# A two-layer graph-attention and expert network: first biases, filler, slots in a row and weight fetches

## The chip, the cores and the metric

One core of one Trainium2 chip runs the whole program. The metric is the device time of one execution in microseconds (us). In the text PE or TensorE is the matrix engine, DVE or VectorE the vector engine, ACT or ScalarE the engine of activation functions, POOL or GpSimd the engine that issues the indirect DMAs, and SP or SyncE the engine that issues the plain DMAs. A name such as L1454 is a line of the kernel before.

## What is computed

Two layers, each an attention over a graph of N = 2708 nodes with D = 256 features, followed by a mixture of 8 experts of which each node uses two:

```python
# layer 0
x = x + gnn0(layernorm(x), adj)      # q k v, masked softmax, elu
x = x + ffn0(layernorm(x))           # top 2 of 8 experts, H = 1024, own norm scale and shift per expert
# layer 1
x = x + gnn1(layernorm(x), adj)      # H = X W + b, scores s_src + s_dst, masked softmax, alpha H
x = x + ffn1(layernorm(x))           # top 2 of 8 experts, H = 512

# one expert
h = gelu(x_e @ W1[e] + b1[e])        # exact gelu
y = h @ W2[e] + b2[e]                # summed over the two experts with the router's weights
```

All inputs and outputs are 32 bit floats; the masks come as a 2708 x 2708 matrix of integers.

## The kernel before

The nodes are cut into NT = 22 tiles of 128 rows. Layer 0's attention goes through six blocks of up to 512 queries (`layer0_attention`); for each of the 22 key tiles of a block it makes scores (L545), exponentials on ScalarE (L557), a product with the mask on VectorE (L560, whose results `p` lie in six buffers), and the sums with the values (L609). At the end of a block the sums are copied (L634, half of them on VectorE), and the remaining steps of a tile (elu, residual, norm, routing) are done piece by piece beside later work through a `Line` of generators.

Routing (`route`) writes each row twice, once for each of its two experts, with an indirect DMA of POOL (L1207) into the DRAM tensor `disp`, sorted by expert. The experts' part is a list of slots of 128 rows of one expert each. There are SURE = 43 slots that are always used, and at most SLOTS = 50. Which expert a slot has is computed at run time (`place`), as a row number (`token_row`) and weight rows (`weight_row`). A slot needs:

- its rows `xg` and their targets and weights `who`, by five DMAs of SP (`fetch_rows`, L1395 and L1401), up to ROWS_AHEAD = 5 slots ahead;
- its expert's weights in one of RING = 4 buffers `ring`, by an indirect DMA of POOL (`fetch_weights`, L1368), AHEAD = 3 slots ahead. Where the buffer holds this expert already, or the slot isn't used, the row number is out of bounds and nothing is moved.

A slot `s` then runs `turned` (rows turned to columns on VectorE, L1436; in layer 0 also scaled and shifted with values from the ring, L1442), `up` (the scaled second bias `bias2`, L1454 on VectorE in layer 0 and L1456 on ScalarE in layer 1; first matmuls L1463; gelu L1471) and `down`, one slot later (second matmuls L1479; weighting and bias, L1485; and an indirect DMA of POOL to the DRAM tensor `xd`, which in layer 0 adds to what is there, L1498, and in layer 1 writes, L1491).

`in_a_row(0, OFTEN)` runs OFTEN = SURE + 2 = 45 slots as straight code in both layers. After it each engine loads the number of used slots (`used`, L1565), and nested branches (L1572) run the other slots one at a time, as far as they are used: `in_a_row(s, s + 1)`. The weights and rows of slots behind the 45th are fetched ahead by the slots before them, whether they turn out to be used or not. The fetch that slot 44 of layer 0 makes for slot 47 waits for the scatter of slot 43 (`behind_add`).

The order of the queues: SP's is written out by hand everywhere. In layer 0's expert part a planner orders PE, ACT, DVE and POOL from the dependencies, by its estimate of when each instruction is ready, and it may put an instruction of the experts among those of the attention. With `tc.issue_after(ins)` the instructions of a block get an edge to `ins`, if they are on its engine: they come behind it in the queue, without a wait for its end. `self.issued` is first the copy L634 of the last block's first tile, and from slot 0's `down` on the last weighting L1485; the transposes L1436 of layer 0 are queued behind it. In layer 1 PE, ACT and DVE keep the order of the code.

Between the layers, `keys_and_values` loads the rows from `xd` (L723), normalises them (L251 to L261), transposes them on PE (L274) and makes the values (L746). Ahead of the first of them PE does `busy(PAUSE)`: 28 products of two constants that nobody reads (L914).

In the profile one product of 32 bit floats is two MATMUL records.

Of the kernel before, what the change touches and what calls it, by code (L numbers as in the profile page):

```python
# [20 lines left out]
P = 128  # L21
# [65 lines left out]
PAUSE = 28  # L87
# [8 lines left out]
OFTEN = SURE + 2  # L96
# [8 lines left out]
def adj_ffn_kernel(ctx: ExitStack, tc: tile.TileContext, a: dict, out: bass.AP):  # L105
# [932 lines left out]
    class Experts:  # L1038
# [327 lines left out]
        def fetch_weights(self, s, behind_add=None):  # L1366
            w, packed = self.ring[s % RING], self.packed_weights[0]
            start = nc.gpsimd.indirect_dma_start(  # L1368
                w, None, packed[:],
                bass.IndirectOffsetOnAxis(ap=self.weight_row[:, s : s + 1], axis=0),  # L1370
                bounds_check=E * P - 1, oob_is_err=False,
            )
            if behind_add is not None:
                tc.add_manual_dep(
                    start.ins, behind_add.ins.name,
                    mybir.DependencyInfo(
                        mybir.DependencyClass.Sync, mybir.DependencyReason.DATA
                    ),
                    reason="no sooner than the results",
                )  # L1380
            return w
# [44 lines left out]
        def slots(self, two, ps_mm, ps_acc, line):  # L1426
            hidden, own_norm, xd = self.hidden, self.own_norm, self.xd
            _, hc, w2, b2, b1, ln, row = self.packed_weights

            def turned(s):  # L1430
# [4 lines left out]
                with tc.issue_after(self.issued.ins) if own_norm and s < OFTEN else ExitStack():  # L1435
                    nc.vector.transpose(  # L1436
                        raw.rearrange("p c (t i) -> p t c i", t=GROUP),
                        xg.rearrange("p t (c j) -> p t c j", c=DC),
                    )
# [9 lines left out]
            def up(w, xe, factor):  # L1449
# [3 lines left out]
                if own_norm:  # L1453
                    nc.vector.tensor_scalar(bias2, w[:, b2:b1], factor, None, ALU.mult)  # L1454
                else:
                    nc.scalar.activation(bias2, w[:, b2:b1], AF.Copy, scale=factor)  # L1456
# [19 lines left out]
            def down(s, w, who, hT, bias2, then):  # L1476
# [24 lines left out]
                if s < FULL_AFTER[self.early]:  # L1501
                    tc.declare_no_dep(start.ins, group=self.groups[3], reason="other rows of xd")
                    tc.add_to_no_dep_group(self.groups[2], start.ins)
                return start
# [6 lines left out]
            def slot(s, s1):  # L1511
# [6 lines left out]
                hT, bias2 = up(w, xe, who[:, 1:2])  # L1518
# [4 lines left out]
                def fetch(behind_add=None):  # L1523
# [4 lines left out]
                    if s + AHEAD < SLOTS and s + AHEAD == len(self.weights):  # L1528
                        self.weights.append(self.fetch_weights(s + AHEAD, behind_add))
                    for _ in range(2):  # L1530
                        at = len(self.rows_)
                        if at <= s + ROWS_AHEAD and at < (SLOTS if placed else n):
                            self.rows_.append(self.fetch_rows(at))
# [7 lines left out]
                if behind is None:  # L1541
                    fetch()
                elif own_norm and s == OFTEN - 1:

                    added = down(*behind, lambda: None)
                    fetch(added)
                else:
                    down(*behind, fetch)
# [5 lines left out]
            def in_a_row(s0, s1):  # L1554
# [8 lines left out]

            in_a_row(0, OFTEN)
            used = nc.values_load(  # L1565
                self.used[0:1, 0:1], min_val=SURE, max_val=SLOTS,
                skip_runtime_bounds_check_because="a sum of rounded-up parts",
            )

            def others(s):  # L1570
                if s < SLOTS:
                    with tc.If(used > s):  # L1572
                        in_a_row(s, s + 1)
                        others(s + 1)

            others(OFTEN)

# [92 lines left out]
```

## Time and profile before

| | us |
|---|---|
| time, median of three runs | 1231.23 (1230.78 to 1231.45) |
| the profiled execution: time | 1228.5 |
| the profiled execution: span from first to last instruction | 1226.7 |
| busy: PE, DVE, ACT, POOL | 1150.6, 565.7, 435.4, 421.3 |
| first matmuls of layer 0's experts | 511.83 |
| last matmuls of layer 0's experts end | 839.87 |
| last result of layer 1's experts begins (L1485) | 1199.02 |
| final sums begin to load (L1625) | 1202.74 |

The times of the last four rows count from the start of the span. Layer 0's 45 slots take 7.03 us each in the steady part, layer 1's 3.51. L1498 was run 45 times and L1491 47 times, so layer 0 used no branch and layer 1 the first two. Idle time of another engine than PE costs nothing by itself; where PE waits, the question is what it waits for. The granted clock of PE is given as a share of full speed.

### The profile page before, as it was taken

Reading aid. Unit: us, or ns where it says so; the run is one execution under the profiler, and the core shown is the slowest. Engines: PE = TensorE matmul, PEld = TensorE weight load, DVE = VectorE, ACT = ScalarE, POOL = GpSimd, SP = SyncE. Lnnn points to the kernel's source line nnn. Section 1 sums busy time; section 2 is a strip of 40 time slices with the busy share of each in tenths; the row PEclk is TensorE's granted clock in tenths of the full one; section 3 lists DMA queues with packets and bytes.
Section 4 is the critical chain, followed back from the end, with each engine's and each line's share of the span. In section 5 each row is a group of like instructions: output and inputs, shape, how many; then the busy total and the mean of one; then the engine's idle time right before and its main releaser. Section 6 shows DMA issues by size and latency. Waiting matters only on the chain. (4 is left out here: it accounts for less than half of the span.)

```text
span 1226.7 us, 20985 instructions
## 1 busy us (share of the span) xinstructions
PE 1150.6 (94%) x6528; PEld 928.7 (76%) x6528; DVE 565.7 (46%) x2147; ACT 435.4 (35%) x1254; POOL 421.3 (34%) x525
## 2 busy tenths in 40 slices
PE   8989999999998999789999999999999998999980
PEld 5656666666665675479999999997899977899880
DVE  5465663754546636352222222223866777422214
ACT  3222222222212212263233233232776757544330
POOL 3011020110211213053433343433654557655450
PEclk9999999999999999799999999999999999999996
DMA  9393973999988494538667966554001527655557
GB/s 205 59 178 69 197 163 101 211 197 235 227 175 202 104 211 193 175 63 258 168 183 207 344 155 176 128 169 105 8 1 41 206 58 202 186 155 141 143 184 278
DMA packets 206252, 198.17 MB, mean 162 GB/s; under 512 B 98027, under 2 KB 189636, under 8 KB 199992
## 3 DMA queue, kind: packets, MB, share of 16 engines
q1 hardware_dynamic: 178202, 110.45, 41.3%
q0 software_dynamic: 27040, 83.56, 21.6%
q10 hardware_dynamic: 894, 2.77, 0.6%
q8 instruction: 54, 0.88, 0.3%
q14 instruction: 62, 0.51, 0.1%
HBM read 263.92 MB, written 66.15 MB: 269 GB/s over the span
## 5 line engine op out<-in xcount | busy, mean ns | idle before, releaser
L1463 PEld LDWEIGHTS mm<-xe,ring 128*128 128x128 f32 x2192 | 261.9, 195 | 23.1 <-issue 7.0
L1463 PE MATMUL mm<-xe,ring 128*128 128x128 f32 x2192 | 267.5, 279 | 12.4 <-DMA ring<-L_ffn_packed,weight_row 4.7
L1479 PE MATMUL acc<-ring,hT 128*128 128x256 f32 x1096 | 255.0, 382 | 4.8 <-ACT hT L1471 4.8
L1471 ACT ACTIVATE hT<-mm,ring 128x128 f32<-128x128 f32 x548 | 156.8, 370 | 280.5 <-issue 156.9
L1479 PEld LDWEIGHTS acc<-ring,hT 128*128 128x128 f32 x1096 | 201.3, 191 | 29.8 <-ACT hT L1471 6.2
L609 PEld LDWEIGHTS acc<-v,p 128*128 128x128 f32 (+1 forms) x880 | 159.5, 190 | 65.7 <-issue 41.0
L609 PE MATMUL acc<-v,p 128*128 128x257 f32 (+1 forms) x880 | 204.1, 384 | 2.8 <-DVE p L560 1.8
L1485 DVE SCALAR_TENSOR_TENSOR y<-acc,who,bias 128x256 f32<-128x256 f32 x92 | 44.4, 483 | 345.6 <-PE acc L1479 337.6
L545 PE MATMUL s<-g,xnT 128*128 128x512 f32 x420 | 202.6, 602 | 0.0
L257 POOL TENSOR_TENSOR ln_rs<-ln_rs,minus_half 128x2 f32<-128x2 f32 x88 | 65.5, 748 | 266.0 <-DVE ln_rs L253 226.4
L1368 POOL DMA_INDIRECT ring<-L_ffn_packed,weight_row x98 | 103.6, 1057 | 145.7 <-PE acc L1479 107.1
L1207 POOL DMA_INDIRECT disp<-row,to x88 | 89.9, 1022 | 162.7 <-DVE to L1204 57.8
L854 PE MATMUL acc<-parts,m 128*128 128x266 f32 x924 | 127.7, 295 | 0.0
L557 ACT ACTIVATE p<-s 128x512 f32<-128x512 f32 x105 | 62.5, 596 | 180.5 <-PE s L545 146.1
L854 PEld LDWEIGHTS acc<-parts,m 128*128 128x128 f32 x924 | 118.3, 187 | 4.4 <-ACT raw L881 0.9
L545 PEld LDWEIGHTS s<-g,xnT 128*128 128x128 f32 x420 | 76.2, 192 | 53.7 <-issue 50.3
L560 DVE SCALAR_TENSOR_TENSOR p<-p,mT 128x512 f32<-128x512 f32 x100 | 68.3, 685 | 94.5 <-ACT p L557 94.4
L1498 POOL DMA_INDIRECT xd<-y,who x45 | 71.3, 1583 | 101.0 <-issue 59.2
L821 ACT CAST m<-mT 128x512 fp32r<-128x512 fp8e4 (+4 forms) x168 | 72.3, 475 | 11.2 <-PE acc L854 7.5
L1491 POOL DMA_INDIRECT xd<-y,who x47 | 47.0, 999 | 22.2 <-issue 11.6
L411 DVE TENSOR_SCALAR m_rows<-adj 128x512 fp8e4<-128x512 int32 (+1 forms) x105 | 42.1, 432 | 2.4 <-DMA adj<-in_adj_dram 2.4
L609 PE MATMUL acc<-v,p_last 128*128 128x257 f32 (+3 forms) x88 | 27.4, 413 | 8.8 <-DVE p_last L560 8.8
(251 smaller groups left out, 1040.8 us busy)
## 6 DMA issues: line engine op xcount, KB each, us to landing
adj<-in_adj_dram SPq DMA_DIRECT2D x100, 256.0 KB
L_ffn_packed<-in_L_ffn_W_dram SPq DMA_DIRECT2D x16, 1024.0 KB
xg<-disp SPq DMA_DIRECT2D x400, 32.0 KB
L_ffn_packed<-in_L_ffn_W_dram SPq DMA_DIRECT2D x16, 512.0 KB
neighbours<-mT SPq DMA_DIRECT2D x5, 1408.0 KB
mT<-neighbours SPq DMA_DIRECT2D x5, 1408.0 KB
xin<-in_x_dram SPq DMA_DIRECT2D x42, 128.0 KB
ring<-L_ffn_packed SPq DMA_DIRECT2D x4, 1154.0 KB
```

The costliest lines, as they stand in the source:

```text
L257: nc.gpsimd.tensor_tensor(rs[:r, 1], rs[:r, 0], minus_half[:r], ALU.pow)
L545: nc.tensor.matmul(ps[:kr, :nb], xnT[:, c, k0 : k0 + kr], g[:, c, :nb], start=(c == 0), stop=(c == DC - 1 and k < KEYS),)
L560: nc.vector.scalar_tensor_tensor(p, p, LARGEST, mask, op0=ALU.min, op1=ALU.mult)
L609: nc.tensor.matmul(accs[j][:r], p[keys, q0 : q0 + r], v[keys, k, :], start=(k == 0), stop=(k == NT - 1),)
L821: nc.scalar.copy(m[:, : q1 - q0], MASKS[b].of_key(mTs[b], k)[:, q0 - b * BN : q1 - b * BN],)
L854: nc.tensor.matmul(acc[:r], masks[t], parts[:, k, i], start=(k == 0 and i == 0), stop=False,)
L1207: nc.gpsimd.indirect_dma_start(disp[:], bass.IndirectOffsetOnAxis(ap=to[:r, j : j + 1], axis=0), rows2[:r, j], None,)
L1368: start = nc.gpsimd.indirect_dma_start(w, None, packed[:], bass.IndirectOffsetOnAxis(ap=self.weight_row[:, s : s + 1], axis=0), bounds_che ...
L1463: nc.tensor.matmul(ps[:, i, :], w[:, c * hidden + f * P : c * hidden + (f + 1) * P], xe[:, c, :], start=(c == 0), stop=(c == DC - 1),)
L1471: nc.scalar.activation(hT[:, f, :], ps[:, i, :], AF.Gelu, bias=w[:, b1 + f : b1 + f + 1])
L1479: nc.tensor.matmul(ps, hT[:, f, :], w[:, w2 + f * D : w2 + (f + 1) * D], start=(f == 0), stop=(f == hc - 1),)
L1498: start = nc.gpsimd.indirect_dma_start(xd[:], at, y, None, bounds_check=N - 1, oob_is_err=False, compute_op=ALU.add)
```

## The change

The queue edge `issue_after(self.issued)` is put on the biases of slots 0 and 1 of layer 0 also, as the transposes have it. The filler PAUSE goes from 28 products to 12, and a second one, BRIDGE, of 8 products stands between the last slot of layer 0 and the branches. The number of slots in straight code is 45 in layer 0 and 47 in layer 1 (`often`). Weights and rows are fetched ahead only for these; a branch fetches its own. The fetch that waited for a scatter is gone with the code for it. In layer 0 the load of `used` on POOL is queued behind the last scatter (`last_start`).

```diff
-PAUSE = 28
+PAUSE = 12
+BRIDGE = 8
...
-OFTEN = SURE + 2
...
-        def fetch_weights(self, s, behind_add=None):
+        def fetch_weights(self, s):
             w, packed = self.ring[s % RING], self.packed_weights[0]
-            start = nc.gpsimd.indirect_dma_start(
+            nc.gpsimd.indirect_dma_start(
...
-            if behind_add is not None:
-                tc.add_manual_dep(
-                    start.ins, behind_add.ins.name,
...
         def slots(self, two, ps_mm, ps_acc, line):
             hidden, own_norm, xd = self.hidden, self.own_norm, self.xd
+            often = SURE + (2 if own_norm else 4)
...
-                with tc.issue_after(self.issued.ins) if own_norm and s < OFTEN else ExitStack():
+                with tc.issue_after(self.issued.ins) if own_norm and s < often else ExitStack():
...
-            def up(w, xe, factor):
+            def up(w, xe, factor, gated):
                 bias2 = two.tile([P, D], F32, name="bias2", bufs=2 if own_norm else 4)
                 if own_norm:
-                    nc.vector.tensor_scalar(bias2, w[:, b2:b1], factor, None, ALU.mult)
+                    with tc.issue_after(self.issued.ins) if gated else ExitStack():
+                        nc.vector.tensor_scalar(bias2, w[:, b2:b1], factor, None, ALU.mult)
...
+                self.last_start = start
                 return start
...
-                hT, bias2 = up(w, xe, who[:, 1:2])
+                hT, bias2 = up(w, xe, who[:, 1:2], own_norm and s < 2)
...
-                    if s + AHEAD < SLOTS and s + AHEAD == len(self.weights):
-                        self.weights.append(self.fetch_weights(s + AHEAD, behind_add))
+                    if len(self.weights) <= s + AHEAD < often:
+                        self.weights.append(self.fetch_weights(s + AHEAD))
                     for _ in range(2):
                         at = len(self.rows_)
-                        if at <= s + ROWS_AHEAD and at < (SLOTS if placed else n):
+                        if at <= s + ROWS_AHEAD and at < (often if placed else n):
                             self.rows_.append(self.fetch_rows(at))
...
-                elif own_norm and s == OFTEN - 1:
-
-                    added = down(*behind, lambda: None)
-                    fetch(added)
...
-            in_a_row(0, OFTEN)
-            used = nc.values_load(
+            in_a_row(0, often)
+            if own_norm:
+                idle = ps_mm.tile([P, GROUP, P], F32, name="mm").rearrange("p g n -> p (g n)")
+                for _ in range(BRIDGE):
+                    nc.tensor.matmul(idle[:, :D], ident, wfc[:, 0, :D], start=True, stop=True)
+            with tc.issue_after(self.last_start.ins) if own_norm else ExitStack():
+                used = nc.values_load(
...
                     with tc.If(used > s):
+                        self.weights.append(self.fetch_weights(s))
+                        self.rows_.append(self.fetch_rows(s))
                         in_a_row(s, s + 1)
                         others(s + 1)
 
-            others(OFTEN)
+            others(often)
```

More of the change, by code (lines that the diff above doesn't have):

```diff
@@ L1372, in fetch_weights @@
             )
-            if behind_add is not None:
-                tc.add_manual_dep(
-                    start.ins, behind_add.ins.name,
[L1376 to L1380, printed above, removed]
             return w
@@ L1521, in slot, with fetch @@
                 line.step()
-                def fetch(behind_add=None):
+                def fetch():
                     for _ in range(2 if s + AHEAD < n else E):
@@ L1561, in in_a_row @@
                 behind = None
-            in_a_row(0, OFTEN)
-            used = nc.values_load(
-                self.used[0:1, 0:1], min_val=SURE, max_val=SLOTS,
-                skip_runtime_bounds_check_because="a sum of rounded-up parts",
-            )
+            in_a_row(0, often)
[5 more added lines that the diff above has]
+                used = nc.values_load(
+                    self.used[0:1, 0:1], min_val=SURE, max_val=SLOTS,
+                    skip_runtime_bounds_check_because="a sum of rounded-up parts",
+                )
             def others(s):
```

## The prediction

> **What bounds the kernel now.** I read the page's table of engines first: TensorE is busy for 1150.6 of 1226.7 us. So time is to be had only where TensorE stands idle, does filler or runs at a lower clock, and the four edits touch three such places: 490 to 511 us (end of layer 0's attention), 840 to 854 us (between the layers) and 1187 to 1200 us (last slots of layer 1). I took each in turn. The waits of 484 to 512 us (columns: total, times, longest):
>
> ```profile
> DVE bias L1454 <- DMA who<-disp: 13.0, 1, 13.0
> PEld acc L609 <- DVE p_last L560: 9.0, 1, 9.0
> PE acc L609 <- DVE p_last L560: 8.8, 1, 8.8
> ```
>
> The timeline of VectorE shows the same hole from its side:
>
> ```profile
> 484.18 0.42 DVE L628 TENSOR_TENSOR x<-neg,xin 128x256 f32<-128x256 f32 x1
> 497.57 0.35 DVE L1454 TENSOR_SCALAR bias<-ring,who 128x256 f32<-128x256 f32 x1 [12.97 <-DMA who<-disp]
> ```
>
> The bias of slot 0 stands in VectorE's queue in the middle of the attention and waits for slot 0's `who`; behind it stand the mask products L560, and behind those the attention's matmuls. Then the windows (PE, PEld, DVE, ACT, POOL busy; granted clock; DMA share; GB/s):
>
> ```profile
> 490.00:498.50 8.50, 0.00 (x0) 0.00 (x0) 0.93 (x4) 0.08 (x1) 0.00 (x0) 0.69 0.78 261
> 498.50:504.00 5.50, 5.47 (x14) 2.62 (x15) 1.53 (x7) 0.29 (x1) 2.11 (x4) 0.55 0.72 200
> ```
>
> The idle time is followed by 5.5 us at about half clock. Why `who` is late shows in the DMA queues between 486 and 489 us:
>
> ```profile
> q0 software_dynamic: 85, 1.20, 95.4%
> q1 hardware_dynamic: 85, 0.02, 3.2%
> ```
>
> The weights of slots 0 to 2 (q0) and the gathered rows (q1) are served one packet for one packet, and a weight packet is 1.20 MB/85 = 14 KB. The three weight fetches end at about 494 us; only then do the small packets flow.
>
> Between the layers, POOL and then PE:
>
> ```profile
> 837.21 1.56 POOL L1498 DMA_INDIRECT xd<-y,who  x1 [4.32 <-DVE y L1485]
> 841.86 1.06 POOL L1368 DMA_INDIRECT ring<-L_ffn_packed,weight_row  x1 [3.08 <-PEq L1572]
> 843.22 1.57 POOL L1498 DMA_INDIRECT xd<-y,who  x1 [0.31 <-issue]
> ```
>
> ```profile
> 841.49 12.32 PE L914 MATMUL acc<-wfc,ident 128*128 128x256 f32 x56 [1.62 <-DVEq L1572]
> 853.65 0.38 PE L274 MATMUL misc<-ident,xn 128*128 128x128 f32 x2
> ```
>
> The chain of waits runs through the whole filler L914. The first normalised tile (L261) was there at 851.60+0.41 = 852.01: the filler is 1.6 us too long, and the data are themselves late by a fetch that sits before the last scatter.
>
> Last slots, PE:
>
> ```profile
> 1188.92 2.05 PE L1463 MATMUL mm<-xe,ring 128*128 128x128 f32 x16 [1.78 <-DVE xe L1436]
> 1191.49 1.99 PE L1479 MATMUL acc<-ring,hT 128*128 128x256 f32 x8 [0.52 <-ACT hT L1471]
> 1194.41 2.05 PE L1463 MATMUL mm<-xe,ring 128*128 128x128 f32 x16 [0.93 <-DVE xe L1436]
> 1196.98 1.99 PE L1479 MATMUL acc<-ring,hT 128*128 128x256 f32 x8 [0.52 <-ACT hT L1471]
> ```
>
> Slots 45 and 46 run in branches, each alone: about 5.5 us apart, where slots in the row take 3.51 us.
>
> [...] 0.55 after 8.8 us of idle, and 1.00 kept over the 1.62 us gap at 840. [...] The scatters L1498 of slots from 24 on keep 4.6 to 4.8 us between starts at their closest[...]. [...] Here TensorE's branch at 837.2 us took 3838 ns, the other engines' 34 to 76 ns.
>
> **Part 1, the first slots' biases behind the attention.** Both now queue behind the copy L634 of the last block. Removed: VectorE's 12.97 us; of it TensorE lost 8.78 us. Also removed: the half clock. Groups that took 2.20, 1.36 and 1.91 us after the hole take 1.14, 0.77 and 1.14 before it: 2.4 us, of which I count 2. The attention thus ends 10.8 us sooner; the copy at 510.23 comes at 499.4. What is late next: `who` of slot 0 was usable at 497.5, so no longer it. But with VectorE free, POOL issues slot 3's weights (L1368, at 500.07 now, behind a 13.46 us wait on VectorE) at about 487. They then follow the others in q0: about 240 packets of token rows, then 128 large ones in about 5.6 us, until 500.4. q1 has 480 packets through by 494, gains 240+128 meanwhile, and needs 512 for slot 0's rows, 640 with its `who`, 1152 for slot 1's rows. So slot 0 is served by about 497, slot 1's rows only at about 503.4 (some 300 packets more at 312/us, and 2 us to land; 498 now). VectorE runs in order:
>
> ```profile
> 510.23 0.43 DVE L634 COPY raw<-acc 128x257 f32<-128x257 f32 x1 [3.14 <-PE acc L609]
> 510.57 0.43 DVE L1436 STREAM_TRANSPOSE xe_raw<-xg 128x256 f32<-128x256 f32 x1
> 510.93 0.11 DVE L297 TENSOR_SCALAR alone<-raw 128x1 f32<-128x1 f32 x1
> 510.97 0.43 DVE L1436 STREAM_TRANSPOSE xe_raw<-xg 128x256 f32<-128x256 f32 x1
> 511.32 0.31 DVE L1442 TENSOR_SCALAR xe<-xe_raw,ring 128x128 f32<-128x128 f32 x1
> ```
>
> If slot 1's transpose still stands ahead of slot 0's L1442, slot 0 waits for slot 1's rows. I take it that the added bias of slot 0 (0.31 us) fills that gap instead and slot 1's transpose comes later. Then slot 0 starts 10.5 us sooner and the hold falls on the routing arithmetic, for which I charge 1.5 us. Bounds: 6.5 us (slot 0 held to about 505, again cold) and 11.5 us (no hold, and fewer of the 1.28 us table switches of ScalarE at 516 to 529). I take **-9.0**. The biases themselves, 2 x 0.35 us, come out of the hole and lie beside matmuls.
>
> **Part 2, between the layers.** The prefetches of slots 45 to 47's weights and of rows past 44 go. The fetch at 841.86 waited for the scatter of slot 43; that of slot 44 must wait for it all the same, so it moves only from 843.22 to about 841.9: 1.3 us. The rows dropped from SP's queue gain nothing: SP was done at 831. The first tile is normalised at 850.7. TensorE: matmuls end at 839.87; 8 bridge matmuls at 12.32/28 = 0.44 us end at 843.4; [...] the second filler starts between 843.4 and 844.9 and, at 12 x 0.44 = 5.3 us, ends between 848.7 and 850.2. Both are before 850.7, so the data decide: transposes at 850.75 to 850.95, not 853.65. **-2.7**, bounds -1.2 (a gap that lowers the clock) and -4. The load of `used` behind the last scatter leaves 0.5 us of POOL's time before it to the other side.
>
> **Part 3, slots 45 and 46 in the row.** No change of fetch times: slot 45's weights landed at 1185.5 (ScalarE waited for them there), TensorE would want them at 1185.2, so 0.3 us are lost. From 1185.5 on: up of 45 (1.78), down of 44 (1.73), up of 46 (1.78), down of 45 and of 46 (1.73 each), 8.75 in all, and 0.1 of waits: the last result comes at 1194.4 instead of 1199.02. **-4.6**; bounds -3 (slot 46's weights, issued at 1182.02, later than now) and -5.2. The scatter, its landing (1199.78 to 1202.74) and the final sums follow unchanged.
>
> **Part 4, branches fetch their own weights.** None is taken: layer 0 scattered 45 times, layer 1 47 times. Skipping costs compare-and-branches on engines that then wait 3 to 4 us for a scatter; POOL's catch-up (INC_SWDGE_SEM, 1.0 and 1.9 us) may grow with more skipped DMAs. Cost 0; up to +2 if this outlasts the scatter's landing, which goes into the range.
>
> Sum: -9.0-2.7-4.6 = -16.3. The profiled execution took 1228.5 us (span 1226.7), so 1212.2 there; the median of the three runs is 1231.23, which gives **1214.9**.
>
> **Rivals.** (a) Slot 1's rows hold slot 0 (the order above; against it, the bias as filler): part 1 gives 6.5, so -13.8: 1217.4. (b) All at the good bounds (fewer table switches, a fully covered gap): -11.5-3.5-5 = -20: 1211. (c) The change doesn't free VectorE, because another instruction with late data takes the bias's place: for it, the planner orders VectorE by estimates and misjudged this `who`; against it, everything else of slots 0 and 1 was queued behind L634 already. -2.7-4.6 = -7.3: 1224. (d) Slower: the new edges and the dropped fetches make the planner order VectorE differently through all of layer 0. There the chain result, transpose, bias, scale ends when TensorE asks for it (829.43 result, 830.80 first matmul, TensorE busy until 831.1), so it has almost no slack. An added 0.43 us operation ahead of the scale costs 43 x 0.43 = 18.5: 1231.2-16.3+18.5 = 1233.4. It decides from 0.38 us a slot on. Against it: slots from 2 on keep their edges.
>
> **Numbers.** Chances: forecast 0.48, (a) 0.22, (b) 0.12, (c) 0.10, (d) 0.08. 1209.5 to 1221.5 holds the first three and leaves out 0.18. A difference under 0.2% (2.5 us) can't be told from none here. Faster 0.90, same 0.02 (the edge of d), slower 0.08.
>
> **What would show it.** No wait of L1454 over 2 us, TensorE busy and at clock 1.00 from 490 to 499; first L1463 at about 501; L1368 of slot 3 near 487; transposes L274 some 2.7 us nearer to the last L1479 of layer 0; 47 slots 3.5 us apart and no gap before the last two. Wrong if first L1463 comes after 506, if layer 0's slots leave 7.03 us, or if slot 45 or 46 waits for weights over 1 us.

## The result and the profile after

The changed kernel takes 1216.95 us (median of 4 runs, 1216.16 to 1218.15), the kernel before 1231.34 beside it (4 runs, 1230.78 to 1233.23): a ratio of 0.988, 95% interval 0.9864 to 0.9898. Two later comparisons, on two different chips, gave 0.986 and 0.985. The profiled execution took 1217.16 us (span 1215.5), that of the kernel before 1228.5, which lay 2.8 us under its own median.

The line numbers of the changed kernel: first matmuls L1457, second L1473, result L1479, bias L1448, transpose L1429, scale L1435, gelu L1465, scatter L1492 in layer 0 and L1485 in layer 1, branches L1568, first filler L1559. L609, L634, L723, L274, L746, L914 and the weights' fetch L1368 keep theirs.

First the end of layer 0's attention. The waits of the changed kernel between 484 and 512 us (columns: total, times, longest):

```profile
DVE p_last L560 <- ACT p_last L557: 5.5, 6, 1.4
...
DVE raw L634 <- PE acc L609: 3.1, 1, 3.1
```

No bias is among them. The windows (PE, PEld, DVE, ACT, POOL busy; granted clock; DMA share; GB/s):

```profile
490.00:498.50 8.50, 8.50 (x47) 4.50 (x46) 1.42 (x6) 1.33 (x5) 0.00 (x0) 1.00 1.07 362
498.50:504.00 5.50, 4.52 (x20) 2.96 (x19) 3.02 (x10) 0.74 (x2) 0.00 (x0) 0.80 0.90 334
```

Where TensorE stood still for 8.5 us it is now busy throughout at clock 1.00. The timeline of VectorE shows the order at the hand-over:

```profile
500.19 0.43 DVE L634 COPY raw<-acc 128x257 f32<-128x257 f32 x1 [3.14 <-PE acc L609]
500.53 0.43 DVE L1429 STREAM_TRANSPOSE xe_raw<-xg 128x256 f32<-128x256 f32 x1
500.89 0.31 DVE L1448 TENSOR_SCALAR bias<-ring,who 128x256 f32<-128x256 f32 x1
501.12 0.34 DVE L1435 TENSOR_SCALAR xe<-xe_raw,ring 128x128 f32<-128x128 f32 x1
```

Slot 0's bias has taken the place in which slot 1's transpose stood; that one now comes at 509.40, and nothing of slot 0 waits for slot 1's rows.

Then the place between the layers, POOL and PE:

```profile
823.43 1.55 POOL L1492 DMA_INDIRECT xd<-y,who  x1 [4.75 <-DVE y L1479]
827.96 1.55 POOL L1492 DMA_INDIRECT xd<-y,who  x1 [2.97 <-DVEq L1568]
```

```profile
830.69 5.42 PE L914 MATMUL acc<-wfc,ident 128*128 128x256 f32 x24 [1.15 <-PEq L1568]
838.56 0.44 PE L274 MATMUL misc<-ident,xn 128*128 128x128 f32 x2 [2.46 <-DVE xn L261]
...
841.10 2.03 PE L746 MATMUL misc<-wfc,xT 128*128 128x273 f32 x4
```

The scatters are 4.5 us apart instead of 6.0, as the dropped fetch lets them be. But the second filler is over at 836.1 and the normalised tile comes only at 838.5: TensorE is idle for 2.46 us, and the four L746 behind it take 2.03 us where four took 1.16 in other traces. The granted clock was 0.74 from 838.5 to 841.0 us and 0.66 from there to 844.1; in the filler ahead of the gap it was 1.00. The last slots of layer 1:

```profile
1176.10 2.02 PE L1457 MATMUL mm<-xe,ring 128*128 128x128 f32 x16 [0.32 <-DMA ring<-L_ffn_packed,weight_row]
1177.96 1.89 PE L1473 MATMUL acc<-ring,hT 128*128 128x256 f32 x8
1181.09 2.02 PE L1457 MATMUL mm<-xe,ring 128*128 128x128 f32 x16 [1.24 <-DMA ring<-L_ffn_packed,weight_row]
1182.95 3.62 PE L1473 MATMUL acc<-ring,hT 128*128 128x256 f32 x16
```

They run in one row now, but slot 46 waits 1.24 us for its weights. The prediction had named a wait of over 1 us there as a sign of being wrong.

To compare traces I cut each span at the same instructions: the first matmuls of layer 0's experts; the result of slot 44, which is the last of layer 0; the second group of L746; the first matmuls of layer 1's experts; the results of slots 41 and 46; the end. All in us, each the difference of two starts in the timeline ("part 1 alone" and so on are the experiments below):

| trace | to first expert | 45 slots of layer 0 | to the values | attention 1 | slots 0-41, layer 1 | slots 41-46 | to the end |
|---|---|---|---|---|---|---|---|
| before | 511.8 | 328.1 | 17.5 | 156.4 | 164.4 | 20.7 | 27.7 |
| before, again | 511.5 | 327.7 | 17.5 | 156.4 | 166.4 | 20.6 | 27.6 |
| changed | 501.7 | 324.4 | 17.9 | 156.7 | 168.1 | 17.8 | 28.9 |
| changed, second trace | 500.6 | 325.1 | 17.9 | 156.6 | 166.6 | 18.0 | 28.7 |
| changed, third trace | 501.3 | 324.6 | 18.0 | 155.4 | 166.2 | 17.5 | 28.7 |
| part 1 alone | 499.3 | 324.4 | 17.5 | 155.5 | 166.4 | 20.7 | 27.8 |
| all but part 1 | 511.3 | 328.8 | 16.9 | 156.5 | 164.5 | 20.1 | 28.6 |
| part 4 alone | 511.1 | 327.6 | 17.5 | 156.4 | 162.4 | 37.3 | 27.4 |

The first two columns carry the gain: 10.2 and 3.6 us in the first pair. The place between the layers gives nothing, the last slots give 2.9 and the end takes 1.2 back. In the slots 0 to 41 of layer 1, which no edit touches, two traces of one kernel differ by 2 us.

### The profile page after: what moved, and what is told of

Same layout as the page of the kernel before. It is cut to its first block, busy times and chain, and to the rows that moved or that the text cites. A ratio compares the mean times of both kernels' runs of the same rounds, so it can differ in the third digit from the quotient of the medians.

```text
span 1215.5 us, 20794 instructions
## 1 busy us (share of the span) xinstructions
PE 1145.4 (94%) x6512; PEld 924.1 (76%) x6512; DVE 566.2 (47%) x2147; ACT 431.9 (36%) x1252; POOL 416.0 (34%) x519
## 3 DMA queue, kind: packets, MB, share of 16 engines
q10 hardware_dynamic: 894, 2.77, 0.6%
## 5 line engine op out<-in xcount | busy, mean ns | idle before, releaser
L1457 PEld LDWEIGHTS mm<-xe,ring 128*128 128x128 f32 x2192 | 259.7, 194 | 26.0 <-issue 11.7
L1457 PE MATMUL mm<-xe,ring 128*128 128x128 f32 x2192 | 265.6, 278 | 14.5 <-DMA ring<-L_ffn_packed,weight_row 7.1
L1473 PE MATMUL acc<-ring,hT 128*128 128x256 f32 x1096 | 254.3, 381 | 1.1 <-issue 1.1
L1465 ACT ACTIVATE hT<-mm,ring 128x128 f32<-128x128 f32 x548 | 156.6, 370 | 273.1 <-issue 168.1
L1473 PEld LDWEIGHTS acc<-ring,hT 128*128 128x128 f32 x1096 | 201.3, 191 | 26.0 <-issue 2.3
L609 PEld LDWEIGHTS acc<-v,p 128*128 128x128 f32 (+1 forms) x880 | 159.7, 190 | 65.2 <-issue 41.0
L609 PE MATMUL acc<-v,p 128*128 128x257 f32 (+1 forms) x880 | 204.6, 384 | 2.3 <-DVE p L560 1.3
L1479 DVE SCALAR_TENSOR_TENSOR y<-acc,who,bias 128x256 f32<-128x256 f32 x92 | 44.4, 482 | 339.2 <-PE acc L1473 322.9
L1207 POOL DMA_INDIRECT disp<-row,to x88 | 90.4, 1027 | 166.2 <-DVE to L1204 58.2
L1368 POOL DMA_INDIRECT ring<-L_ffn_packed,weight_row x92 | 97.6, 1060 | 128.3 <-PE acc L1473 88.4
L1492 POOL DMA_INDIRECT xd<-y,who x45 | 71.8, 1595 | 118.7 <-issue 70.4
L1485 POOL DMA_INDIRECT xd<-y,who x47 | 47.1, 1002 | 23.6 <-issue 11.0
L417 DVE STREAM_TRANSPOSE mT<-m_rows 128x128 int32<-128x128 int32 x100 | 33.4, 393 | 0.1
```

What stands on the lines that cost most here:

```text
L609: nc.tensor.matmul(accs[j][:r], p[keys, q0 : q0 + r], v[keys, k, :], start=(k == 0), stop=(k == NT - 1),)
L1207: nc.gpsimd.indirect_dma_start(disp[:], bass.IndirectOffsetOnAxis(ap=to[:r, j : j + 1], axis=0), rows2[:r, j], None,)
L1368: nc.gpsimd.indirect_dma_start(w, None, packed[:], bass.IndirectOffsetOnAxis(ap=self.weight_row[:, s : s + 1], axis=0), bounds_check=E * P ...
L1457: nc.tensor.matmul(ps[:, i, :], w[:, c * hidden + f * P : c * hidden + (f + 1) * P], xe[:, c, :], start=(c == 0), stop=(c == DC - 1),)
L1465: nc.scalar.activation(hT[:, f, :], ps[:, i, :], AF.Gelu, bias=w[:, b1 + f : b1 + f + 1])
L1473: nc.tensor.matmul(ps, hT[:, f, :], w[:, w2 + f * D : w2 + (f + 1) * D], start=(f == 0), stop=(f == hc - 1),)
```

## The experiments

Each was timed beside the kernel before on the same chip. There the kernel before took 1228.56 us (the first four kernels), 1227.96 (the next four) and 1230.09 (the last four).

**The kernel before, once more**, unedited.

> The kernel before, unchanged, profiled a second time. In its first profile layer 1's slots run from the first L1463 (1013.85) to the result of slot 41 (1178.27) in 164.4 us; in the profile of the changed kernel the same stretch takes 168.1 us (1000.71 to 1168.79) though nothing in it was edited. Theory (spread of one kernel in its weight waits): the stretch differs here from 164.4 by 2 us or more, towards 168, and ratio 1.000. Rival (the change lengthens it): 164.4 within 1 us again.

It took 1227.67 us, ratio 0.9996 (0.9984 to 1.0008). Its trace gives the spread between executions: only the slots 0 to 41 of layer 1 moved by more than 0.4 us (166.4 against 164.4). TensorE's waits for weights in layer 1's experts summed to 6.9 us here and 4.7 in the first trace, and to 7.1, 11.0 and 10.2 in the three of the changed kernel. A difference of some 2 us in that stretch can therefore not be put down to an edit. The waits for weights alone do not order it either: the changed kernel took 168.1 us with 7.1 us of such waits and 166.6 with 11.0.

**Part 1 alone**, in the kernel before:

```diff
-            def up(w, xe, factor):
+            def up(w, xe, factor, gated):
...
-                    nc.vector.tensor_scalar(bias2, w[:, b2:b1], factor, None, ALU.mult)
+                    with tc.issue_after(self.issued.ins) if gated else ExitStack():
+                        nc.vector.tensor_scalar(bias2, w[:, b2:b1], factor, None, ALU.mult)
...
-                hT, bias2 = up(w, xe, who[:, 1:2])
+                hT, bias2 = up(w, xe, who[:, 1:2], own_norm and s < 2)
```

> Kernel before with only the edge on the biases of slots 0 and 1. Theory (all that layer 0 gained comes from it, the planner's other order of ScalarE with two table switches fewer included): first matmuls of the experts near 501.7, last result of layer 0 near 826.1 instead of 839.9, time 13.8 us below before, 1217.5. Rival (the fewer table switches come from the other edits): 10.2 us, 1221.1. Rival of the prediction (slot 1's rows hold slot 0): 6.5 us.

1212.91 us, ratio 0.9864 (0.984 to 0.9889), some 16 us: all that the whole change brings. Beside the 12 us ahead of the first expert (10 to 11 in the traces of the whole change) the 45 slots take 3.7 us less. Where these are, the results of slots 0, 1 and 2 show, first of the kernel before and then of the changed one (timeline of VectorE):

```profile
527.81 0.48 DVE L1485 SCALAR_TENSOR_TENSOR y<-acc,who,bias 128x256 f32<-128x256 f32 x1 [4.17 <-PE acc L1479]
...
539.89 0.48 DVE L1485 SCALAR_TENSOR_TENSOR y<-acc,who,bias 128x256 f32<-128x256 f32 x1 [0.22 <-PE acc L1479]
...
547.44 0.48 DVE L1485 SCALAR_TENSOR_TENSOR y<-acc,who,bias 128x256 f32<-128x256 f32 x1 [4.32 <-PE misc L1189]
```

```profile
518.98 0.47 DVE L1479 SCALAR_TENSOR_TENSOR y<-acc,who,bias 128x256 f32<-128x256 f32 x1
...
526.42 0.48 DVE L1479 SCALAR_TENSOR_TENSOR y<-acc,who,bias 128x256 f32<-128x256 f32 x1 [3.71 <-PE acc L1473]
...
533.88 0.48 DVE L1479 SCALAR_TENSOR_TENSOR y<-acc,who,bias 128x256 f32<-128x256 f32 x1 [4.28 <-PE misc L1189]
```

From the first matmul to slot 0's result it is 1.3 us more (17.3 against 16.0), but slot 1 follows after 7.4 us instead of 12.1. In the kernel before, ScalarE and PE were doing this in between:

```profile
526.17 1.28 ACT L622 ACT_TABLE_LOAD   x1
...
528.21 1.28 ACT L1471 ACT_TABLE_LOAD   x1
529.50 2.18 ACT L1471 ACTIVATE hT<-mm,ring 128x128 f32<-128x128 f32 x8
...
529.92 2.13 PE L1479 MATMUL acc<-ring,hT 128*128 128x256 f32 x6 [2.15 <-ACT hT L1471]
```

The second matmuls waited 2.15 us for gelus that stood behind two loads of ScalarE's tables, after 0.92 us for the same reason at 524.92. Between 490 and 548 us the kernel before has nine such loads of 1.28 us, the changed one seven. That count goes with part 1 in all fourteen traces: seven in the ten with the edge on the biases, nine in the four without. A switch costs its load alone here: the one at 528.21 ends at 529.49 and the gelu begins at 529.50. Two loads fewer are thus 2.6 us of ScalarE by the trace. That these are behind the 3.6 us is argued from the waits; no kernel changed them alone.

**All but part 1**: the changed kernel with the biases free.

```diff
-                hT, bias2 = up(w, xe, who[:, 1:2], own_norm and s < 2)
+                hT, bias2 = up(w, xe, who[:, 1:2], False)
```

> The change without its first part: the biases of slots 0 and 1 are not tied to the attention's end. Theory: the first matmul of layer 0's experts starts at 511.8 us again instead of 501.7 or sooner, and the stretch from there to slot 44's result takes 328 us instead of 324.4, since ScalarE loads its tables nine times instead of seven while routing and first slots mix: 13.8 us above the changed kernel beside it. Rival, the 3.5 us in the stretch come from elsewhere in the change (the branches' own fetches, which leave the queue of weights shorter) and not from the order of the first slots: 10 us above, with 324.4 in the stretch. Second rival, the filler and the row of 47 give by themselves what they were meant to, and the three parts do not add: under 8 us above.

1226.42 us, against 1212.48 for the changed kernel on the same chip: 13.9 us more, the first theory's 13.8. The two columns went back to 511.3 and 328.8, so the 3.6 us in the slots belong to the bias edge and not to the branches' own fetches. Its ratio to the kernel before is 0.9987 (0.9968 to 1.0006): parts 2, 3 and 4 together are worth 1.5 us by the medians and can't be told from nothing. In its trace the row of 47 gave only 0.6 us in the slots 41 to 46: slot 46 waited 2.36 us for its weights, and its first matmuls then took 2.84 us instead of 2.02. The same came once more among the nine traces with the row of 47 (the weights ahead, below: a wait of 2.46 us, 20.1 us for the stretch).

**A second filler of 18** in the changed kernel (`PAUSE = 18`), and **the weights ahead in layer 0**, where the weights of slots 45 to 47 are fetched in the row again. In the changed kernel each of the five branches of layer 0 (slots 45 to 49) holds the fetch of its own weights. With the weights ahead two weight fetches are left in the branches, those of slots 48 and 49, as in the kernel before.

```diff
-                    if len(self.weights) <= s + AHEAD < often:
+                    if len(self.weights) <= s + AHEAD < (SLOTS if own_norm else often):
...
-                        self.weights.append(self.fetch_weights(s))
+                        if s == len(self.weights):
+                            self.weights.append(self.fetch_weights(s))
```

> Changed kernel with PAUSE 18 instead of 12. Theory (the short filler ends 2.5 us before the first normalised tile, the clock falls, and the matmuls up to 844 run at half speed for 1.7 us more): filler ends at about 838.6, where the tile is ready, clock stays at 1.00, time 1.5 to 2 us below the changed kernel, 1215.2. Rival (the data alone decide): no difference, 1217. Rival (the filler becomes the bound): slower by up to 1 us.

> Changed kernel, but in layer 0 the weights of slots 45 to 47 are fetched ahead by the slots before them, as in the kernel before (without the wait on a scatter), and the first three branches fetch rows only. In the changed kernel POOL goes from its branch (828.8) to the catch-up of skipped DMAs (831.9) in 3.1 us, before the change in 1.1 us, and SP's loads wait for it. Theory (the code of the weight fetches in the branches makes POOL's skip longer): 2 us from branch to catch-up or less, first load L723 4.3 to 5 us after the last scatter instead of 6.0, time 0.5 to 1.7 us below the changed kernel. Rival (the number of skipped row DMAs or the new order of the queue makes it): 3.1 us still, no difference.

1209.4 us (ratio 0.9841, 0.9815 to 0.9867) and 1211.93 (0.9863, 0.9838 to 0.9887); the changed kernel did not run beside them, so the traces are what they are read by. What stands in the queue of POOL for the line of the branches, and in that of SP for the line of the loads, in the changed kernel and then with the weights ahead (count; shortest, median, longest in ns; first and last start in us):

```profile
L1568 POOLq EVENT_SEMAPHORE  x4: 17/43/43, 829.3 to 831.8; - x4
...
L1568 POOLq COMPARE_BRANCH  x1: 53/53/53, 828.8 to 828.8; - x1
L1568 POOLq INC_SWDGE_SEM  x1: 940/940/940, 831.9 to 831.9; - x1
```

```profile
L723 SPq EVENT_SEMAPHORE  x12: 17/28/28, 832.8 to 833.9; - x12
```

```profile
L1568 POOLq EVENT_SEMAPHORE  x3: 42/43/43, 829.2 to 829.4; - x3
...
L1568 POOLq COMPARE_BRANCH  x1: 53/53/53, 828.7 to 828.7; - x1
L1568 POOLq INC_SWDGE_SEM  x1: 1010/1010/1010, 829.5 to 829.5; - x1
```

```profile
L723 SPq EVENT_SEMAPHORE  x12: 17/28/977, 830.5 to 832.5; - x12
```

POOL skips the branches, waits for a few semaphores (EVENT_SEMAPHORE) and then comes to INC_SWDGE_SEM, the catch-up. In the changed kernel all eight semaphores of POOL's DMAs (110 to 117) rise once at its end, from 832.70 to 832.76 us, with no DMA landing; I take these rises for the skipped DMAs. There the catch-up comes 3.0 us after the branch, and SP, which loads the rows for layer 1, goes on at its end (831.9+0.94 = 832.8). With the weights ahead it comes 0.8 us after the branch, and SP then waits for the scatter itself, as the chain of waits of that kernel shows:

```profile
827.89 3.71 DMA xd<-y,who
831.62 0.07 issue
831.68 0.03 SPq L723
```

The scatter lands 3.71 us after its start and releases SP. So the fetches moved into the branches take the first load from 4.7 to 6.0 us behind the scatter.

What POOL waits for, the numbers of the semaphores in the traces tell. The last scatter of the changed kernel raises semaphore 116 when it lands. Of POOL's four waits ahead of the catch-up the second stands at 829.39; the third names 116 and stands at 831.70, 3.74 us behind the scatter's start. With the weights ahead the last scatter raises 111; the waits and the catch-up name the other seven of POOL's eight semaphores (110 and 112 to 117), and none of them is held up. In all nine traces whose branches hold five or three weight fetches the last scatter's semaphore is in this list, and the instruction that names it stands 3.6 to 3.8 us behind the scatter's start; in all five traces with two it is not (in the kernel before it is 111, and the catch-up raises the other seven from 845.34 to 845.41 us), and the catch-up comes 0.8 to 1.6 us behind it.

The fetch of slot 47's weights costs something too where it stands in the row: the last scatter comes 2.6 us after slot 44's result instead of 1.8.

TensorE with the weights ahead, then with the filler of 18:

```profile
837.12 0.44 PE L274 MATMUL misc<-ident,xn 128*128 128x128 f32 x2 [1.57 <-DVE xn L261]
...
839.53 1.16 PE L746 MATMUL misc<-wfc,xT 128*128 128x273 f32 x4 [0.33 <-DMA kept<-xd]
```

```profile
837.74 0.44 PE L274 MATMUL misc<-ident,xn 128*128 128x128 f32 x2
...
840.11 1.16 PE L746 MATMUL misc<-wfc,xT 128*128 128x273 f32 x4 [0.30 <-DMA kept<-xd]
```

(The second fence is from the repeat of the filler of 18 below.) Without the gap, or with one of 1.57 us, L746 keeps its 1.16 us, and the load is followed by the values after 9.1 us instead of 10.1. From slot 44's result to the values it took 16.3 us with the weights ahead, 16.7 with the longer filler, 17.9 in the changed kernel, 17.5 before.

**The weights ahead in both layers and a second filler of 15**: as in the edit above with `SLOTS` for both layers, and `PAUSE = 15`.

> Theory: between the layers the changed kernel's POOL takes 3.1 us to skip the branches because each holds a fetch of weights, and TensorE's gap of 2.5 us before the first transposes of the attention lowers its clock. With the weights fetched ahead of the branches (in both layers) and a second filler of 15, POOL's skip takes about 0.8 us, the kept rows' first load follows the scatter by 4.7 us instead of 6.0, the gap is under 1 us and L746 runs at 1.16 us: from the last result of layer 0 to the second group of values about 16.3 us against 17.9, 1.6 less. At the end the first final load follows the last scatter by 2.96 us instead of 3.40 and the rest takes 0.6 less. Sum 2.5 us under the changed kernel beside it. Rival, the skip is not what holds the loads (the scatter's landing is): the loads still follow by 5.9 us, and the gain is that of the filler alone, 1 us or less.

1209.91 us, 2.6 under the changed kernel on the same chip, but the ratios are 0.9863 (0.9836 to 0.989) and 0.9864 (0.9835 to 0.9893): not told apart. The trace gave the expected parts between the layers (16.6 us; load 4.8 us after the scatter; gap 0.34 us; L746 1.16 us). At the end it did not: 28.7 us as in the changed kernel, so the branches' fetches are not what makes the end longer.

**The row of 45 in layer 1**, with that layer's weights and rows fetched ahead as before:

```diff
-            often = SURE + (2 if own_norm else 4)
+            often = SURE + 2
+            ahead = often if own_norm else SLOTS
...
-                    if len(self.weights) <= s + AHEAD < often:
+                    if len(self.weights) <= s + AHEAD < ahead:
...
-                        if at <= s + ROWS_AHEAD and at < (often if placed else n):
+                        if at <= s + ROWS_AHEAD and at < (ahead if placed else n):
...
-                        self.weights.append(self.fetch_weights(s))
-                        self.rows_.append(self.fetch_rows(s))
+                        if own_norm:
+                            self.weights.append(self.fetch_weights(s))
+                            self.rows_.append(self.fetch_rows(s))
```

> Layer 1 as it was before: 45 slots in a row, slots 45 and 46 in branches, weights and rows fetched ahead of them; all else as changed. Theory: the row of 47 is worth what the stretch from the result of slot 41 to that of slot 46 shows (20.7 before, 17.8 and 17.1 with the row of 47), so this kernel takes 20.7 there again, 3.2 us more, and gets 0.4 us back in the wait for the final loads and 0.6 in the last stretch, since its branches hold no fetch: about 2.2 us above the changed kernel. Rival, the wait for slot 46's weights only moves (TensorE waits for weights in other slots of the stretch instead): the stretch from slot 0 to slot 41 of layer 1 gives back what the last five slots cost, and the two kernels are within 0.8 us.

1213.32 us, 0.8 above the changed kernel beside it (ratio 0.988, 0.9853 to 0.9908): by time neither theory falls. By the stretches: the slots 41 to 46 took 20.6 us (18.0 beside it), the end 27.5 (28.7), the slots 0 to 41 164.8 (166.6). The first is worth 2.6 us to the row of 47 and the second takes 1.2 of it back. The 1.2 us at the end go with the row of 47 in every trace: 28.4 to 28.9 us in nine with it, 27.4 to 27.8 in five without. Some 0.4 us of it lie between slot 46's result and the first of the final loads; the cause stays open.

**Two weights ahead**: in layer 0 the weights of slots 45 and 46 in the row, so that the branches of slots 47 to 49 hold one fetch each, a filler of 15, and in layer 1 the rows of slots 47 to 49 fetched ahead.

```diff
-                    if len(self.weights) <= s + AHEAD < often:
+                    if len(self.weights) <= s + AHEAD < (often + 2 if own_norm else often):
...
-                        if at <= s + ROWS_AHEAD and at < (often if placed else n):
+                        if at <= s + ROWS_AHEAD and at < ((often if own_norm else SLOTS) if placed else n):
...
-                        self.weights.append(self.fetch_weights(s))
-                        self.rows_.append(self.fetch_rows(s))
+                        if s == len(self.weights):
+                            self.weights.append(self.fetch_weights(s))
+                        if s == len(self.rows_):
+                            self.rows_.append(self.fetch_rows(s))
```

> The changed kernel with a second filler of 15, in layer 0 the weights of slots 45 and 46 fetched in the row of 45 and only slot 47's in its branch, and in layer 1 slot 47's rows (not its weights) fetched in the row. Theory: three fetches in skipped branches cost POOL 3.1 us and none 0.8, so one costs about 1.5; slot 47's fetch no longer stands ahead of the last scatter, which comes 1.8 us after slot 44's result as in the changed kernel (2.6 where all weights were fetched ahead); the first kept load then follows the scatter by its landing, 4.6 us, not by POOL's skip, and the values by 9.1: 15.5 us from slot 44's result to the second group of values, against 17.9 for the changed kernel and 16.6 with all ahead. Rival, every fetch left in a branch holds POOL for more than its share: 5.3 us or more from the scatter to the load, sum 16.2 or more. At the end, if the rows fetched in the branch are what makes the last stretch 24.6 us instead of 23.9, it is 23.9 here; if not, 24.5.

The theory fell, the rival held: the load came 5.8 us after the scatter, 16.6 us in all. Its queues of POOL and SP, by the same two lines:

```profile
L1568 POOLq EVENT_SEMAPHORE  x4: 17/43/43, 828.8 to 829.0; - x4
...
L1568 POOLq COMPARE_BRANCH  x1: 53/53/53, 828.3 to 828.3; - x1
L1568 POOLq INC_SWDGE_SEM  x1: 980/980/980, 831.1 to 831.1; - x1
```

```profile
L723 SPq EVENT_SEMAPHORE  x12: 17/28/28, 832.0 to 833.1; - x12
```

Three fetches in the branches delay POOL about as five do (2.8 us from the branch to the catch-up, 3.0 in the changed kernel), so it is no work per fetch. Nor does POOL merely stop at a fixed place of its list. Here the last scatter raises semaphore 110, which none of the four waits names, but the catch-up itself: the four are over by 829.1 us, and the catch-up comes at 831.1, 3.7 us behind the scatter's start (827.40). In both orders POOL stops at the instruction that names the last scatter. Only 0.95 us later does SP go on. With three or five fetches in the branches the list holds all eight of POOL's semaphores, with two all but the last scatter's. In the row POOL's DMAs have the eight in turn (the kernel before, 815.61 to 843.22 us: 111 to 117, 110, 111). My guess is that the skipped ones have them in turn too, since two fetches and five scatters make seven; no run changed the number of DMAs alone, so this is not shown.

The time was 1209.1 us (0.9841, 0.9814 to 0.9868), the lowest on its chip, not told apart from the changed kernel (1212.64, 0.9846) beside it.

**Part 4 alone**: the kernel before, with its long filler and its rows of 45, whose branches fetch their own weights and rows.

```diff
-                    if s + AHEAD < SLOTS and s + AHEAD == len(self.weights):
+                    if s + AHEAD < OFTEN and s + AHEAD == len(self.weights):
...
-                        if at <= s + ROWS_AHEAD and at < (SLOTS if placed else n):
+                        if at <= s + ROWS_AHEAD and at < (OFTEN if placed else n):
...
+                        self.weights.append(self.fetch_weights(s))
+                        self.rows_.append(self.fetch_rows(s))
                         in_a_row(s, s + 1)
```

> The kernel before with the change's fourth part alone: slots 45 to 47 fetch their own weights and rows in their branches, in both layers; fillers, biases and the row of 45 as before. Theory: the skip of the branches takes POOL 3.1 us instead of 1.05 in layer 0, but the long filler keeps TensorE's clock up and reaches to 853.65 us, so most of it hides: the kept rows' load follows the scatter by 5.9 instead of 4.2 us, load to values gives back what TensorE waited less, 1 us at most, sum 17.6 to 19 instead of 17.5; the scatter itself comes up to 1.5 us sooner, since the fetch of slot 47's weights is not ahead of it. In layer 1 both branches of 45 and 46 are taken and each now waits for its weights from memory, issued only in the branch: from the result of slot 41 to that of slot 46 some 8 us more for each of the two, 30 to 38 us instead of 20.7. So about 15 us above the kernel before, and nearly all of it in layer 1. Rival, a fetch in a branch is as early as one in the row, because the sequencers of POOL and SP run ahead of TensorE through the branches: at most 4 us above.

1245.77 us, ratio 1.0133 (1.0105 to 1.0161), 15.7 above the kernel before. In layer 0 it costs nothing: the load is 5.8 us behind the scatter, the scatter 1.4 sooner, and with the filler of 28 over all of it the stretch is 17.5 us as before. In layer 1, where the two branches are taken, the slots 41 to 46 take 37.3 us. POOL and PE:

```profile
1186.06 1.05 POOL L1368 DMA_INDIRECT ring<-L_ffn_packed,weight_row  x1 [0.52 <-DVE xe L1436]
1199.08 0.99 POOL L1491 DMA_INDIRECT xd<-y,who  x1 [11.97 <-DVE y L1485]
1200.38 1.05 POOL L1368 DMA_INDIRECT ring<-L_ffn_packed,weight_row  x1 [0.30 <-issue]
```

```profile
1192.01 3.75 PE L1463 MATMUL mm<-xe,ring 128*128 128x128 f32 x16 [8.24 <-DMA ring<-L_ffn_packed,weight_row]
...
1206.23 3.61 PE L1463 MATMUL mm<-xe,ring 128*128 128x128 f32 x16 [7.95 <-DMA ring<-L_ffn_packed,weight_row]
```

Each fetch is issued only in its branch, behind the scatter of the slot before, and TensorE waits about 8 us for it. Part 4 is thus free only where the branch is skipped. By these figures the changed kernel would pay this for a 48th slot; these inputs don't use one.

**The changed kernel twice more, and the filler of 18 beside it.**

> The changed kernel as it is, as the one beside which the three other runs are read. It took 0.988 of the kernel before in its first comparison, 14.4 us less. Of two earlier runs one had only the gate on the biases and took 0.986, the other had the whole change with a second filler of 18 and took 0.984, on a chip where the changed kernel itself was not run. If nothing but spread between chips lies behind that, this run takes 0.986 +- 0.002, above the run with the filler of 18 by about 1 us.

> The changed kernel as it is, as the one beside which these three are read: 0.987 of the kernel before, from its two comparisons so far (0.988 and 0.986). Between the layers 17.9 us, POOL's skip 3.1 us, as in its two traces; the waits for weights in layer 1 differ from trace to trace (7.1 and 11.0 us of TensorE's time so far).

> The changed kernel with a second filler of 18 matmuls instead of 12, beside the changed kernel on one chip. The traces gave 1.2 us less between the layers (16.7 against 17.9). Theory: 1.2 us under the changed kernel. Rival, the filler's 1.4 us push the start of the values where no gap threatened: no difference. A difference above 3 us is spread of layer 1's weights, not the filler.

The changed kernel took 1212.48 us (0.9864, 0.9835 to 0.9893) and 1212.64 (0.9846, 0.9816 to 0.9876). The filler of 18 took 1211.74 (0.9846, 0.982 to 0.9871) beside the latter: 0.9 less by the medians, 1.1 less between the layers by the traces (16.9 against 18.0), nothing by the ratio. In both new traces of the changed kernel the gap ahead of the transposes is there, 2.7 and 2.8 us, with 1.28 and 1.83 us for the four L746.

## Why the prediction was right, and which of its terms were not

The forecast was 1214.9 us, the median is 1216.95: inside the range, and the forecast case by its mechanisms: the bias blocked VectorE, and freeing it gave the gain. That the sum came so near is luck, since two errors largely cancel: part 1 gave 4.8 us more than its term, and parts 2 to 4 gave 6.0 less than theirs (1.3 instead of 7.3).

**Part 1**, put at -9.0 with bounds of -6.5 and -11.5, gave -13.8 in the first pair (10.2+3.6), outside the bounds, and 13.9 when it was undone. Its first step held: the copy L634 came at 500.19 (499.4 predicted), the first expert at 501.67 (some 501), slot 3's weights were issued at 488.74 (near 487), and the bias did fill the gap in which slot 1's transpose stood. The charge of 1.5 us for routing arithmetic showed as the 1.3 us more to slot 0's result. What was missing stood only among the bounds, as fewer table switches: the new order of the first slots gives 4.6 us back at slot 1.

**Part 2**, put at -2.7 with bounds of -1.2 and -4, gave +0.4, outside the bounds too. The term that failed is the arrival of the data, "the first normalised tile at 850.7". It let the kept rows' load follow the scatter as before, in 4.2 us, and the load followed in 6.0. Slot 44's result is 13.8 us sooner in the changed trace, so the predicted scatter stands at 828.1 (827.96 measured), the end of the second filler, estimated from TensorE's branch of 3838 ns, at or before 836.4 (836.1, the branch took 3597 ns) and the transposes at 837.0: they came at 838.56, only 1.3 us nearer to the last L1473 of layer 0 and not 2.7.

From slot 44's result to the values the 0.4 us come apart as -1.5 (the scatter, put at -1.3), +1.7 (from the scatter to the load) and +0.2 (from the load to the values, 10.14 us instead of 9.95). The last was to be -1.4. The transposes did follow the first tile at once, where the long filler had held them for 1.6 us. But from the first transpose to the values it then took 5.5 us instead of 3.75. Of this 0.7 us are the tiles: they come 1.2 us apart, and behind the long filler the second one lay ready; without a low clock the stretch takes 4.5 us with a short filler (two weights ahead, 837.63 to 842.10). The prediction had no such term. The other 1.0 us is the lower clock behind the gap (0.74 from 838.5 to 841.0 us, 0.66 to 844.1). In the kernel before the granted clock was 0.55 behind 8.8 us of idle and 1.00 over the gap of 1.62 us at 840. How long a gap lowers it the traces do not settle: the stretch took 5.5 us behind gaps of 2.10, 2.46, 2.68 and 2.77 us, but 4.5 behind 2.20 and 1.57, and behind 2.20 (all but part 1) the first four L746 took 1.16 us, as without a gap. In each of these traces another gap of 0.9 to 1.4 us lies ahead of the filler, 5.4 us before.

**Part 4**, put at 0 with "up to +2 if this outlasts the scatter's landing", is where most of the 1.7 us between scatter and load come from. The outlasting was named and priced, but left out of the likeliest case, since skipping was thought of as work on engines that wait anyway. It is a wait for the landing, and the 0.95 us of the catch-up then stand behind it: 1.3 us against the run with the weights ahead. The other 0.5 us (4.7 us there, 4.2 in the kernel before) lie in SP's queue between the landing and the first load, and stay open. In the kernel before it would have been free (part 4 alone: 17.5 us), because the filler of 28 reached past it; the same change that shortened the filler took that cover away.

**Part 3**, put at -4.6 with -3 as a bound "slot 46's weights, issued at 1182.02, later than now", gave -2.9 in the slots 41 to 46. The size is that of the bound, but its reason is not what happened: slot 46's weights were issued at 1172.54, 3.75 us behind slot 41's result, as in the kernel before. They took 8.5 us from there to TensorE (1181.09), while a fetch with no other weights in flight took 6.0 (1186.06 to 1192.01, part 4 alone). The prediction's sum needs them 10.7 us behind slot 41's result (1185.5+1.78+1.73 = 1189.0, against 1178.27); they came 12.3 behind it, and these 1.6 us are the shortfall of 1.7 within rounding. I had read slot 45's arrival as the last wait. "The scatter, its landing and the final sums follow unchanged" failed as well: 28.9 us against 27.7. Net 1.7.

**The rivals.** (a) fell with the order of VectorE, (c) with the windows, and (d) too: from slot 2's result to slot 44's both kernels take 292.2 to 292.5 us (839.91-547.44 and 826.12-533.88), so no operation was added to layer 0's steady chain. (b), whose sum takes 3.5 and 5 where the bounds are 4 and 5.2, was right on the table switches and wrong on the gap. The sum of the first pair is -13.8+0.4-2.9+1.2 = -15.1 for the four places, and +3.7 and +0.2 from slots 0 to 41 of layer 1 and attention 1: the -11.2 of the two spans (1226.7 to 1215.5).

## What to carry to other kernels

An instruction that waits for data must not stand in an in-order queue ahead of work that could run: here a bias of 0.35 us held VectorE for 12.97 us and TensorE for 8.78 of them, and one queue edge on it gave all of the measurable gain. A short piece of filler shows a delay of the data that a longer one hid (2.46 us of idle TensorE behind 12 products, none behind 28), so look at what feeds the next stage before shortening it, and price each edit of a change with the cover that the other edits leave it. A DMA moved into a branch was not free here when the branch was skipped: ahead of the catch-up POOL waited for earlier DMAs, for the last scatter where its semaphore is in the list (3.0 us from the branch to the catch-up instead of 0.8), and SP, which waits for the skipped ones, waited for all of this too (its first load came 6.0 us behind the scatter instead of 4.7). When the branch was taken, the latency of the DMA lay bare: TensorE waited 8.24 and 7.95 us.

## What the runs showed that was not expected

- POOL's catch-up after skipped branches waits for the last scatter's landing (3.7 to 4.0 us after its start) in the nine traces where three or five weight fetches stand in the branches and the scatter's semaphore is among those waited for; in the five traces with two fetches it is not, and the catch-up comes after 0.8 to 1.6 us. Within the changed kernels the load of the rows starts 1.0 to 1.3 us later for it.
- A weight fetch issued in a taken branch kept TensorE waiting for 8.24 and 7.95 us; from its issue to the first matmul it took 6.0 us alone and 8.5 in the row with others.
- Layer 1's slots 0 to 41 differ by 2.0 us between two executions of the kernel before, and by 3.9 us between the two of the changed kernel with the filler of 18, on two chips (163.9 and 167.8). TensorE's waits for weights sum to 4.2 to 11.0 us (part 4 alone apart), but do not order these stretches by themselves.
- The final loads and sums take 1.1 us longer behind a row of 47 slots than behind a row of 45 and two branches, in fourteen traces without exception.
